# Half of a recurrent state transposed on VectorE and through DRAM instead of on TensorE, with five PSUM banks for gates and one for transposes

## The chip, the cores and the metric

The kernel runs on one core of a Trainium2 chip. The metric is device time in microseconds (us) of one execution. Three executions of the kernel before gave 2820.95, 2821.49 and 2822.5 us; the median is 2821.49 us. A further execution was profiled: its program took 2821.51 us and the span of its records, on which all sums below are made, is 2819.7 us.

## The reference, cut to what matters

There are B = 128 graphs of N = 128 nodes with D = 256 features, in float32. Three attention layers come first (each: layer norm, ReLU, masked softmax attention, ELU, added to the input), then one gated graph layer of three steps. The change lies in the gated layer alone:

```
h = relu(layernorm(x))
A = (adj != 0)
for i in range(3):
    m    = h @ weight[i]                      # 128 x 256 per graph
    aggr = A.T @ m                            # messages summed over neighbours
    gi, gh = aggr @ w_ih.T + b_ih, h @ w_hh.T + b_hh
    r = sigmoid(i_r + h_r); z = sigmoid(i_z + h_z)
    n = tanh(i_n + r * h_n)
    h = (1 - z) * n + z * h
x = x + h
```

The kernel multiplies `weight[i]` into `w_ih` once at the start (`wc`), so that a step is: sum `h` over neighbours (`ag`), then products of `ag` with `wc` and of `h` with `w_hh`, then the gates.

## The kernel before, in words

**Tiling.** The 128 graphs are cut into 33 groups: 2 graphs, 31 times 4 graphs, 2 graphs (`SIZES`, line 213). A group of 4 graphs has 512 columns, one PSUM bank of float32. The state `h` is kept with features on the partitions, in two halves of 128 features (`h0`, `h1`; the code's `k` where it is read and `c` where it is written), each 128 x 512.

**One gated step** (`step`, line 738). The products with weights take `h` as it lies. The sum over neighbours needs the nodes on the partitions, so for steps 1 and 2 each half is transposed first: `node_major` (line 726) makes one TensorE transpose per graph into a PSUM bank `hnp`, ScalarE copies the bank to `hn` (line 762), four TensorE products of `hn` with the adjacency `am` fill the bank `agp` (line 773), and VectorE copies it to `ag` (line 781). For step 0 the node-major state is there already (`hn0`). In `half(c)` (line 784) each half of the new state takes four gate banks: `nn`, `r` and `z` start from `h` and `whh`, `r` and `z` are finished with `ag` and `wc`, `ni` is made from `ag` and `wc` alone (all line 751). ScalarE and VectorE then form the gates, and the last VectorE instruction (line 840) writes the new half `h`. All of half 0 precedes half 1 in the gate arithmetic, so `h0` of a step is ready some 10 us before `h1`.

**PSUM.** The eight banks are shared out in line 231: two for attention (`gat`), four for gates and for the setup's products (`gru`), two for transposes and neighbour sums (`tr`).

**Transposes without TensorE.** The kernel already has one such way, `exchanged` (line 428): VectorE transposes the 32 x 32 blocks of a tile, one DMA writes the result to DRAM, and four DMAs (one for each 32 partitions) read the blocks back in their new places. It serves the attention weights (`tr_at`, `d_at`, `at`), the first state of a group (`tr_h`, `d_h`, `h`) and the last (`tr_o`, `d_o`, `o`), for the groups that `far` selects; the groups at the ends use TensorE.

**Order of the work.** Nothing is ordered by hand. Every instruction is given to a planner (`Plan`, line 40) with its engine, a cost, a rank and what it reads and writes. The planner lets the engines run in simulated time; whenever one is free it takes, of the instructions that could start within 0.1 us of the earliest, the one of lowest rank (lines 132 to 140). A buffer ring (an SBUF tag, a PSUM tag) holds an instruction back until its slot is free. A DMA costs SyncE 0.45 us and its data are taken to land a stated time later: the first argument of `load`. The result is one fixed order for each engine, TensorE's, VectorE's, ScalarE's and SyncE's (which issues all DMAs); on the chip each engine goes through its order and waits on semaphores. So a landing time in the code delays nothing by itself: it decides where the instructions that need the data are put. Ranks rise by 3 for each group; attention of a later group has a rank near that of the gated steps of an earlier one, and its TensorE work is what stands between the gated steps. Gate arithmetic is ranked 2 ahead (`quick`).

**Start.** Weights are transposed and multiplied on TensorE while the attention of the first two groups begins: `attention_weights` (line 280) forms `va` by VectorE products (line 294), TensorE transposes `vp` (line 299) and a ScalarE copy (line 306); the attention scores (line 483) wait for `va`. `mask` (line 316) transposes the node mask `nm` (line 320), and `transposed` (line 328) the weights (line 338).

Of the kernel before, what the change touches and what calls it, by code (L numbers as in the profile page):

```python
# [8 lines left out]
FT = mybir.dt.float32  # L9
# [5 lines left out]
P = 128  # L15
# [24 lines left out]
class Plan:  # L40
# [15 lines left out]
    def load(self, lands, rank, fn, **keys):  # L56

        op = self.add("SP", 0.45, rank, fn, **keys)
        op.lands = lands
        return op  # L60

    def add(self, engine, cost, rank, fn, reads=(), writes=(), after=(), takes=()):


        reads = [k if isinstance(k, tuple) else (k, None) for k in reads]
        writes = [k if isinstance(k, tuple) else (k, None) for k in writes]
        vals = list(dict.fromkeys(v for v, _ in reads + writes))
        vals += [v for v in dict.fromkeys(takes) if v not in vals]
        op = Op(engine, cost, rank, fn, vals)
        for v in vals:  # L70
            v.ops.append(op)

        def others(book, key):
            for part, ops in book.get(key[0], {}).items():
                if part is None or key[1] is None or part == key[1]:
                    yield from ops

        for key in reads:
            for d in others(self.writers, key):
                op.deps[d] = True  # L80
        for key in writes:
            for book in (self.writers, self.readers):
                for d in others(book, key):
                    op.deps.setdefault(d, False)
        for d in after:
            op.deps.setdefault(d, False)
        for v, part in writes:
            w, r = self.writers.setdefault(v, {}), self.readers.setdefault(v, {})
            if part is None:
                w.clear()  # L90
                r.clear()
            else:
                r.pop(part, None)
            w[part] = [op]
        for v, part in reads:
            if (v, part) not in writes:
                self.readers.setdefault(v, {}).setdefault(part, []).append(op)
        for d in op.deps:
            d.users.append(op)
        self.ops.append(op)  # L100
        return op
# [80 lines left out]
def kernel(  # L182
# [25 lines left out]
    nc = tc.nc  # L208
    B, N, D = x.shape
    KD = D // P  # L210
    G = 4
    FAR = 2
    SIZES = [2] + [G] * ((B - 4) // G) + [2]
    NG = len(SIZES)
# [13 lines left out]
    setup = ExitStack()  # L228
    su = setup.enter_context(tc.tile_pool(name="setup", bufs=2))
    rw_pool = []  # L230
    BANKS = {"gat": 2, "gru": 4, "tr": 2}

    plan = Plan()
    add, load = plan.add, plan.load
# [4 lines left out]
    def val(pool, tag, shape, name, bufs=2, dtype=FT, cut=None):  # L239

        def make():
            if pool is None and not rw_pool:
                setup.close()
                rw_pool.append(ctx.enter_context(tc.tile_pool(name="rw", bufs=2)))
            p = rw_pool[0] if pool is None else pool
            t = p.tile([P, *shape], dtype, tag=tag, name=name, bufs=bufs)
            return t if cut is None else t[:, :cut]
        return plan.val(pool, tag, bufs, make)
# [10 lines left out]
    def dve(cols):  # L259
        return 0.12 + cols / 1000  # L260

    def act(cols):
        return 0.25 + cols / 1400
# [52 lines left out]
    def mask():  # L316
        nm = val(su, "nm", [N], "nm")
        nmp = bank("gat", "nmp")
        load(2.6, SETUP, lambda: nc.sync.dma_start(nm.t[:B], nodemask), writes=[nm])
        add("PE", 0.11, SETUP, lambda: nc.tensor.transpose(nmp.t[:, :B], nm.t[:B], ident[:B, :B]),  # L320
            reads=[nm], writes=[nmp])
        add("ACT", act(P), SETUP, lambda: nc.scalar.copy(nmT.t, nmp.t[:, :B]),
            reads=[nmp], writes=[nmT])
# [4 lines left out]
    def transposed(src, dst, name):  # L328
        rows = src.shape[0] // P
        ld = val(su, "wld", [O3 // P, D], f"{name}_ld")  # L330
        load(2.6, SETUP, lambda: nc.sync.dma_start(
            ld.t[:, :rows], src.rearrange("(r p) d -> p r d", p=P)), writes=[ld])

        def part(k, r0, n):
            ps = bank("gru", f"{name}_{k}_{r0}")

            def turn(r):
                add("PE", 0.11, SETUP, lambda: nc.tensor.transpose(
                    ps.t[:, r * P : (r + 1) * P], ld.t[:, r0 + r, k * P : (k + 1) * P], ident
                ), reads=[ld], writes=[(ps, r)], takes=[dst])  # L340

            for r in range(n):
                turn(r)
            add("ACT", act(n * P), SETUP, lambda: nc.scalar.copy(
                dst.t[:, k, r0 * P : (r0 + n) * P], ps.t[:, : n * P]
            ), reads=[ps], writes=[(dst, (k, r0))])

        for k in range(KD):
            for r0 in range(0, rows, 4):
                part(k, r0, min(4, rows - r0))  # L350
# [77 lines left out]
    def exchanged(srcs, cut, dst, name, n, rank):  # L428

        kd = len(srcs)
        f = kd * n * 32
        tr = val(gw, f"tr{kd}", [Q, kd * G * 32], f"tr_{name}")
        d = plan.val(
            dram, f"d{kd}_{n}", 2,
            lambda: dram.tile([Q, 32, Q, f], FT, tag=f"d{kd}_{n}", name=f"d_{name}"),
        )

        def blocks(k):  # L440
            add("DVE", dve(n * P), rank, lambda: nc.vector.transpose(
                tr.t[:, :, :f].rearrange("p j (k b c) -> p k b j c", k=kd, b=n)[:, k],
                cut(k).rearrange("p b (j r) -> p b j r", j=Q),
            ), reads=[srcs[k]], writes=[(tr, k)], takes=[d, dst])

        for k in range(kd):
            blocks(k)
        load(2.8 if kd == 1 else 3.8, rank, lambda: nc.sync.dma_start(
            d.t.rearrange("q r j f -> (q r) j f"), tr.t[:, :, :f]), reads=[tr], writes=[d])

        def back(j):
            load(2.8 if kd == 1 else 3.8, rank, lambda: nc.sync.dma_start(
                dst.t[j * 32 : (j + 1) * 32, :, :f], d.t[:, :, j, :].rearrange("q r f -> r q f")
            ), reads=[d], writes=[(dst, j)])

        for j in range(Q):
            back(j)
# [246 lines left out]
    def gru(g, xt, am, hn0, h0):  # L704
# [7 lines left out]
        def state(tag, name, bufs=2):  # L712
            return val(None, tag, [T], name, bufs=bufs)
# [12 lines left out]
        def node_major(name, hv, k, rank, to):  # L726
            ps = bank("tr", f"hnp_{name}_{k}")

            def turn(b):
                add("PE", 0.11, rank, lambda: nc.tensor.transpose(  # L730
                    ps.t[:, b * P : (b + 1) * P], hv.t[:, b * P : (b + 1) * P], ident
                ), reads=[hv], writes=[(ps, b)], takes=[to])

            for b in range(n_g):
                turn(b)
            return ps

        def step(i):
            name = f"{g}_{i}"
            rank = 3.0 * g + i  # L740
            quick = rank - URGENT
            ag = [state(f"ag{k}", f"ag_{name}_{k}") for k in range(KD)]
            hn = [state(f"hn{k}", f"hn_{name}_{k}") for k in range(KD if i > 0 else 0)]

            def product(ps, c, w, v, k, start, stop, at, takes=(), after=after):
                def fn():
# [10 lines left out]
            def aggregate(k):  # L757

                if i > 0:
                    hv = hn[k]  # L760
                    hp = node_major(name, h[k], k, rank + 0.1 * k, hv)
                    add("ACT", act(TG), quick, lambda: nc.scalar.copy(hv.t[:, :TG], hp.t[:, :TG]),  # L762
                        reads=[hp], writes=[hv])
                ps = bank("tr", f"agp_{name}_{k}")
                t = ag[k]

                def part(b):
                    def fn():
                        if i > 0:
                            s = hv.t[:, b * P : (b + 1) * P]  # L770
                        else:
                            s = hn0.t[:, b, k * P : (k + 1) * P]
                        nc.tensor.matmul(  # L773
                            ps.t[:, b * P : (b + 1) * P], s, am.t[:, b, :], start=True, stop=True
                        )
                    add("PE", pe(P), rank + 0.1 * k, fn,
                        reads=[hv if i > 0 else hn0, am], writes=[(ps, b)], after=after, takes=[t])

                for b in range(n_g):
                    part(b)  # L780
                add("DVE", dve(TG), quick, lambda: nc.vector.tensor_copy(t.t[:, :TG], ps.t[:, :TG]),  # L781
                    reads=[ps], writes=[t])

            def half(c):
# [44 lines left out]
                def difference():  # L829
# [10 lines left out]
                add("DVE", dve(TG), quick, lambda: nc.vector.scalar_tensor_tensor(  # L840
                    hc.t[:, :TG], d.t[:, :TG], 0.5, n.t[:, :TG], op0=OP.mult, op1=OP.add
                ), reads=[d, n], writes=[hc])
                return hc

            return [half(c) for c in range(KD)]
# [78 lines left out]
```

## Time and profile before

| engine | busy us | share of the span | instructions |
|---|---|---|---|
| TensorE, matmuls | 2763.2 | 98% | 10021 |
| VectorE | 2142.3 | 76% | 5622 |
| ScalarE | 1234.5 | 44% | 2627 |
| GpSimd | 293.0 | 10% | 369 |
| 16 DMA engines, mean (queue of SyncE's DMAs) | | 22.5% | 197104 packets |

The page names engines by short names: PE is TensorE, PEld its weight loads, DVE VectorE, ACT ScalarE, SP SyncE. Every float32 product appears as two PE instructions, a transpose as one. The duration of a PE instruction includes latency that overlaps its neighbours: 792 instructions of 580 ns in each of six groups are more than the span holds. What one costs is read from the distance between the starts of successive ones in the timeline.

The granted TensorE clock is 0.994 of full speed over the span. In windows, PE is busy 59.05 of the first 90 us, 48.29 of the next 60, 147.65 of the 150 after that, 696.13 of 300 to 1000 us, all of 1000 to 2700 us, and 52.28 of the last 60 us.

### The profile page before, as it was taken

How to read it: one execution, taken by the hardware profiler on the slowest of the kernel's cores; microseconds unless marked ns; L12 is line 12 of the kernel's file. 1: busy time of each engine (PE TensorE's matmuls, PEld its weight loads, DVE VectorE, ACT ScalarE, POOL GpSimd, SP SyncE). 2: the span in 40 equal slices, each digit the busy share in tenths (PEclk: the TensorE clock that was granted, in tenths of full speed). 3: DMA queues.
4: the chain of work that ended last, by engine and by line, in shares of the span. 5: the costliest groups of instructions: out<-in, count | busy, mean ns of one | idle time of the engine just before them, and what ended most of it. 6: DMA issues, size and time to landing. Idle time of an engine off the chain costs nothing.

```text
span 2819.7 us, 32353 instructions
## 1 busy us (share of the span) xinstructions
PE 2763.2 (98%) x10021; PEld 1615.4 (57%) x10021; DVE 2142.3 (76%) x5622; ACT 1234.5 (44%) x2627; POOL 293.0 (10%) x369
## 2 busy tenths in 40 slices
PE   6889999999999999999999999999999999999998
PEld 4755555555555555555555555555555555555556
DVE  6879888778787778777778777777777787776543
ACT  4444444444444444444444444444444444444322
POOL 1111111101110101110110110110110110100000
PEclk9999999999999999999999999999999999999999
DMA  3123212222212222112222122222122222122100
GB/s 100 38 67 87 77 51 83 75 79 79 56 50 75 77 78 79 49 56 75 75 79 75 50 60 75 71 79 76 48 62 77 72 79 70 40 58 60 47 30 12
DMA packets 197277, 185.24 MB, mean 66 GB/s; under 512 B 33776, under 2 KB 165872, under 8 KB 197104
## 3 DMA queue, kind: packets, MB, share of 16 engines
q1 hardware_dynamic: 197104, 183.17, 22.5%
q8 instruction: 79, 1.29, 0.2%
q14 instruction: 94, 0.77, 0.1%
HBM read 109.65 MB, written 73.46 MB: 65 GB/s over the span
## 4 chain that ended last, share of the span: by engine, by line
PE 93%; DVE 5%; DMA 1%; ACT 1%; issue 0%; SPq 0%; POOL 0%; DVEq 0%; ACTq 0%
PE r L751 22%; PE z L751 22%; PE hp L614 11%; PE ni L751 11%; PE nn L751 11%; PE ahp L595 6%; PE agp L773 6%; PE hnp L730 2%; DVE scr L483 1%; PE wcp L370 0%; DVE st L413 0%; DVE em L525 0%; DVE xo L630 0%; DVE xo L632 0%; DMA whh_ld<-in_L_gnn_w_hh_dram 0%
## 5 line engine op out<-in xcount | busy, mean ns | idle before, releaser
L751 PE MATMUL nn<-h,whh 128*128 128x512 f32 (+1 forms) x792 | 395.8, 581 | 10.2 <-DMA h<-d_h 8.4
L751 PE MATMUL r<-ag,wc 128*128 128x512 f32 (+1 forms) x792 | 397.0, 583 | 2.5 <-DVE ag L781 2.5
L751 PE MATMUL z<-ag,wc 128*128 128x512 f32 (+1 forms) x792 | 394.3, 579 | 0.0
L751 PE MATMUL r<-h,whh 128*128 128x512 f32 (+1 forms) x792 | 394.2, 580 | 0.0
L751 PE MATMUL ni<-ag,wc 128*128 128x512 f32 (+1 forms) x792 | 394.1, 579 | 0.0
L751 PE MATMUL z<-h,whh 128*128 128x512 f32 (+1 forms) x792 | 394.1, 579 | 0.0
L614 PE MATMUL hp<-w,ah 128*128 128x256 f32 x1536 | 363.3, 382 | 0.2
L808 ACT ACTIVATE r<-r,brz 128x512 f32<-128x512 f32 (+1 forms) x198 | 133.1, 672 | 483.7 <-PE r L751 483.2
L614 PEld LDWEIGHTS hp<-w,ah 128*128 128x128 f32 x1536 | 281.1, 191 | 40.3 <-ACT ah L602 5.3
L483 DVE SCALAR_TENSOR_TENSOR scr<-xn,va 128x256 f32<-128x256 f32 x732 | 265.9, 422 | 29.5 <-ACT xn L475 28.6
L811 DVE SCALAR_TENSOR_TENSOR n<-r,wn 128x512 f32<-128x512 f32 (+1 forms) x198 | 132.6, 669 | 179.0 <-ACT r L808 178.5
L751 PEld LDWEIGHTS r<-ag,wc 128*128 128x128 f32 x792 | 148.2, 190 | 186.6 <-issue 155.3
L751 PEld LDWEIGHTS r<-h,whh 128*128 128x128 f32 x792 | 150.4, 190 | 178.2 <-issue 174.9
L751 PEld LDWEIGHTS z<-h,whh 128*128 128x128 f32 x792 | 149.9, 190 | 177.5 <-issue 158.2
L773 PEld LDWEIGHTS agp<-am,hn 128*128 128x128 f32 x1536 | 203.4, 191 | 57.8 <-issue 37.8
L751 PEld LDWEIGHTS ni<-ag,wc 128*128 128x128 f32 x792 | 145.6, 190 | 147.8 <-issue 128.7
L628 ACT ACTIVATE t<-hp 128x512 f32<-128x512 f32 x192 | 104.4, 594 | 286.9 <-PE hp L614 283.5
L751 PEld LDWEIGHTS z<-ag,wc 128*128 128x128 f32 x792 | 145.6, 190 | 147.3 <-issue 145.9
L773 PE MATMUL agp<-am,hn 128*128 128x128 f32 x1536 | 208.8, 276 | 4.9 <-ACT hn L762 3.6
L751 PEld LDWEIGHTS nn<-h,whh 128*128 128x128 f32 x792 | 142.6, 191 | 121.9 <-issue 105.9
L525 DVE SCALAR_TENSOR_TENSOR em<-er,e,cap 128x128 f32<-128x128 f32 x366 | 156.8, 484 | 67.6 <-DMA er<-de 67.6
L494 POOL TENSOR_SCALAR xo<-xo 128x1024 f32<-128x1024 f32 (+1 forms) x66 | 73.3, 1111 | 1292.6 <-DMA out_dram<-xo 589.3
(90 smaller groups left out, 3662.3 us busy)
## 6 DMA issues: line engine op xcount, KB each, us to landing
er<-de SPq DMA_DIRECT2D x90, 256.0 KB, 4.1
d_at<-tr_at SPq DMA_DIRECT2D x90, 256.0 KB, 2.0
at<-d_at SPq DMA_DIRECT2D x360, 64.0 KB, 2.0
x<-in_x_dram SPq DMA_DIRECT2D x31, 512.0 KB, 4.0
d_h<-tr_h SPq DMA_DIRECT2D x31, 512.0 KB, 4.9
h<-d_h SPq DMA_DIRECT2D x124, 128.0 KB, 3.4
out_dram<-xo SPq DMA_DIRECT2D x31, 512.0 KB, 2.9
d_o<-tr_o SPq DMA_DIRECT2D x30, 512.0 KB, 4.3
```

Source lines behind the costliest of these rows:

```text
L483: add("DVE", dve(D), rank, lambda: nc.vector.scalar_tensor_tensor(scr.t, xn.t[:, b, :], 1.0 if far else rs.t[:, b : b + 1], VA[l].t[:, s, ...
L494: add("POOL", 0.14 + n * D / 1070, rank, lambda: nc.gpsimd.tensor_scalar(xo.t, xt.t, 1.0, -1.0, op0=OP.mult, op1=OP.add), reads=[xt], writ ...
L525: add("DVE", dve(P) + (0.15 if far else 0.05), rank, lambda: nc.vector.scalar_tensor_tensor(em.t[:, b, :], e2_row(b), e.t[:, 0, b : b + 1] ...
L595: add("PE", pe(P), rank, lambda: nc.tensor.matmul(summed(ps, b), xn.t[:, b, k * P : (k + 1) * P], turned_weights(b), start=True, stop=True ...
L614: add("PE", pe(D), rank, lambda: nc.tensor.matmul(hp.t[:, b * D : (b + 1) * D], ah.t[:, k, c * P : (c + 1) * P], W[l].t[:, k, :], start=(k ...
L628: power = add("ACT", act(T), rank, lambda: nc.scalar.activation(t.t, hp.t, AF.Exp), reads=[hp], writes=[t])
L730: add("PE", 0.11, rank, lambda: nc.tensor.transpose(ps.t[:, b * P : (b + 1) * P], hv.t[:, b * P : (b + 1) * P], ident), reads=[hv], writes ...
L751: nc.tensor.matmul(o, w.t[:, k, c * P : (c + 1) * P], m, start=start, stop=stop)
L773: nc.tensor.matmul(ps.t[:, b * P : (b + 1) * P], s, am.t[:, b, :], start=True, stop=True)
L808: add("ACT", act(TG) + 0.1, quick, lambda: nc.scalar.activation(r.t[:, :TG], pr.t[:, :TG], AF.Tanh, bias=brz.t[:, cr : cr + 1], scale=0.5) ...
L811: add("DVE", dve(TG), quick, lambda: nc.vector.scalar_tensor_tensor(n.t[:, :TG], r.t[:, :TG], 1.0, wn.t[:, :TG], op0=OP.add, op1=OP.mult), ...
```

## The change

Five edits are made.

1. Of six PSUM banks that gates and transposes share, gates get five instead of four and transposes one instead of two.
2. A new function, `turned_state`, transposes one half of the state without TensorE: one VectorE transpose of 32 x 32 blocks (128 x 512), one DMA of 256 KB to DRAM in pieces of 512 B, four DMAs of 64 KB back, one for each 32 partitions, in pieces of 128 B. The planner is told 3.0 us for the landing of the first and 6.0 us (`LANDS`) for each of the four.
3. It is called at the end of half 0 of steps 0 and 1, for groups 2 to 30 (all of four graphs): 58 times.
4. Where it was called, the next step leaves out the four TensorE transposes of half 0, their PSUM bank and the ScalarE copy. Half 1 goes as before, and so do groups 0, 1, 31 and 32.
5. In the setup, the planner is told other landing times: 8.0 us instead of 2.6 for the node mask, 8.0 for the two large weights and 4.0 for the three small ones, instead of 2.6.

```diff
+    LANDS = 6.0
-    BANKS = {"gat": 2, "gru": 4, "tr": 2}
+    BANKS = {"gat": 2, "gru": 5, "tr": 1}
...
-        load(2.6, SETUP, lambda: nc.sync.dma_start(nm.t[:B], nodemask), writes=[nm])
+        load(8.0, SETUP, lambda: nc.sync.dma_start(nm.t[:B], nodemask), writes=[nm])
...
-        load(2.6, SETUP, lambda: nc.sync.dma_start(
+        load(8.0 if rows > KD else 4.0, SETUP, lambda: nc.sync.dma_start(
             ld.t[:, :rows], src.rearrange("(r p) d -> p r d", p=P)), writes=[ld])
...
+    def turned_state(src, dst, name, n, rank):
+        tr = val(gw, "trs", [G, P], f"tr_{name}", cut=n)
+        d = plan.val(
+            dram, f"ds_{n}", 2, lambda: dram.tile([n, P, P], FT, tag=f"ds_{n}", name=f"d_{name}")
+        )
+        add("DVE", dve(n * P), rank, lambda: nc.vector.transpose(
+            tr.t.rearrange("p b j -> p (b j)"), src.t[:, : n * P]
+        ), reads=[src], writes=[tr], takes=[d, dst])
+        load(3.0, rank, lambda: nc.sync.dma_start(d.t.rearrange("b p f -> p b f"), tr.t),
+            reads=[tr], writes=[d])
+        def back(j):
+            load(LANDS, rank, lambda: nc.sync.dma_start(
+                dst.t[j * 32 : (j + 1) * 32, : n * P].rearrange("c (m r) -> c m r", r=32),
+                d.t[:, :, j * 32 : (j + 1) * 32].rearrange("b (q c) r -> c (b q) r", q=Q),
+            ), reads=[d], writes=[(dst, j)])
+        for j in range(Q):
+            back(j)
...
+        ahead = []
...
-            hn = [state(f"hn{k}", f"hn_{name}_{k}") for k in range(KD if i > 0 else 0)]
+            hn = [
+                ahead[0] if k == 0 and ahead else state(f"hn{k}", f"hn_{name}_{k}")
+                for k in range(KD if i > 0 else 0)
+            ]
...
-                    hp = node_major(name, h[k], k, rank + 0.1 * k, hv)
-                    add("ACT", act(TG), quick, lambda: nc.scalar.copy(hv.t[:, :TG], hp.t[:, :TG]),
-                        reads=[hp], writes=[hv])
+                    if k == 0 and ahead:
+                        ahead.clear()
+                    else:
+                        hp = node_major(name, h[k], k, rank + 0.1 * k, hv)
+                        add("ACT", act(TG), quick, lambda: nc.scalar.copy(
+                            hv.t[:, :TG], hp.t[:, :TG]), reads=[hp], writes=[hv])
...
+                if c == 0 and i < STEPS - 1 and FAR <= g < NG - FAR:
+                    ahead.append(state("hn0", f"hn_{g}_{i + 1}_0"))
+                    turned_state(hc, ahead[0], f"hn_{g}_{i + 1}", n_g, quick)
                 return hc
```

## The prediction

> **What bounds the kernel now.** I read the page's first part and its chain of work first, then the PE timeline of one group from the middle, then the waits of PE, then the start. Engine shares and the chain:
>
> ```profile
> PE 2763.2 (98%) x10021; PEld 1615.4 (57%) x10021; DVE 2142.3 (76%) x5622; ACT 1234.5 (44%) x2627; POOL 293.0 (10%) x369
> PE 93%; DVE 5%; DMA 1%; ACT 1%; issue 0%; SPq 0%; POOL 0%; DVEq 0%; ACTq 0%
> ```
>
> A busy PE need not be PE at its peak, so the next view must show it. In the PE timeline the distance between starts is what an instruction costs. At the first hand-over between two gated steps of one group:
>
> ```profile
> 1390.18 1.02 PE L751 MATMUL nn<-h,whh 128*128 128x512 f32 x2
> 1391.05 1.02 PE L751 MATMUL r<-h,whh 128*128 128x512 f32 x2
> 1391.90 1.02 PE L751 MATMUL z<-h,whh 128*128 128x512 f32 x2
> 1392.76 0.60 PE L730 MATMUL hnp<-ident,h 128*128 128x128 f32 x4
> 1393.20 1.46 PE L614 MATMUL hp<-w,ah 128*128 128x256 f32 x6
> 1394.50 1.05 PE L773 MATMUL agp<-am,hn 128*128 128x128 f32 x8
> 1395.39 2.32 PE L614 MATMUL hp<-w,ah 128*128 128x256 f32 x10
> 1397.55 1.02 PE L751 MATMUL nn<-h,whh 128*128 128x512 f32 x2
> ```
>
> The reader is to see that no line has an idle time: attention work (hp) fills the hand-over. A gate product takes 0.86 us from start to start, four transposes 0.44 us (1392.76 to 1393.20), a neighbour sum 0.89, sixteen hp 3.46, sixteen ahp 1.79. A group of four graphs needs 72 gate products (61.9), 3 times 16 hp (10.4) and 16 ahp (5.4), six neighbour sums (5.3) and four sets of transposes (1.8): 84.8 us. The chain of work in order of time shows successive groups 84.9 us apart (ahp at 1364.34, again at 1449.24). So between about 300 and 2700 us **PE's throughput sets the time**, with nothing to spare: 1 us of PE work less per group is 1 us less, if PE is still never kept waiting.
>
> The start is different. Its waits, of PE and of DVE:
>
> ```profile
> PE nmp L320 <- DMA nm<-in_nodemask_dram: 13.3, 1, 13.3
> PE nn L751 <- DMA h<-d_h: 8.4, 1, 8.4
> DVE scr L483 <- ACT va L306: 8.5, 1, 8.5
> ```
>
> PE's first instruction, the mask's transpose, waits until 13.29 us for its load, and the first transpose of whh until 15.45. The four vp transposes that va needs stand behind them, though their inputs were made on DVE by 9.3 us (timeline); so DVE idles from 11.3 to 19.87. The 8.4 us later on is group 1's first state, which comes late out of the same stretch.
>
> **What the Trainium skill says.** "TensorE: Matmul & The Clock Gate", Part 4 (PE-mode transpose), gives about 275 ns for a transpose in a kernel's context; the trace has 273, but only 0.11 us of each is PE's own time here, and that is what I use. "VectorE: DVE Perf Modes", The three transpose paths, says that VectorE transposes 32 x 32 blocks only, so blocks must be moved by something else: in this kernel already by DMAs (tr_at, d_at, at). "DMA: Bandwidth & Descriptors", Specifications, states that pieces under 512 B cause read-modify-write. The trace of before doesn't show it as a delay: at<-d_at lands 2.0 us after issue both with 512 B pieces (64 KB) and with 256 B pieces (32 KB). The same page, Anatomy of one DMA, says that a DMA's wait is made on the issuing sequencer; the trace agrees, SyncE waiting 123.1 us in 89 waits for d_at before it issues at.
>
> **The change part by part.** Rows used:
>
> ```profile
> L730 PE MATMUL hnp<-ident,h 128*128 128x128 f32 x524 | 79.6, 273 | 3.0 <-DVE h L840 3.0
> L762 ACT COPY hn<-hnp 128x512 f32<-128x512 f32 x124 | 72.0, 581 | 123.0 <-PE hnp L730 122.9
> L441 DVE STREAM_TRANSPOSE tr_at<-em 128x512 f32<-128x512 f32 x90 | 64.0, 711 | 3.0
> d_at<-tr_at SPq DMA_DIRECT2D x90, 256.0 KB, 2.0
> at<-d_at SPq DMA_DIRECT2D x360, 64.0 KB, 2.0
> out_dram<-xo SPq DMA_DIRECT2D x31, 512.0 KB, 2.9
> ```
>
> *Removed from PE.* 29 groups, two hand-overs each, four transposes: 232 of 524. 58 x 0.44 = **25.5 us**, all in the stretch where PE sets the time. The group's period goes from 84.9 to 84.0 us.
>
> *Removed from ACT.* 58 copies of 0.58 us, 34 us. ACT is 44% busy; counted as nothing.
>
> *Added on DVE.* 58 x 0.71 = 41 us, 76% to 78% of the span. Each is ranked with the gates, so it stands behind h0 and ahead of half 1's gate arithmetic; what it delays by 0.7 us is h1 or an attention step. At the hand-over shown h1 was written at 1393.2 and first used at 1397.55, so 4 us of attention work on PE cover it. Counted as nothing.
>
> *Added on SyncE and the DMA engines.* A write takes 0.34 us to issue and four reads 1.75 us (timeline, L448 and L452): 58 x 2.1 = 121 us of SyncE. Queued behind the new wait for the write are de, er, at and the loads of x and adj; DVE's em waits for er, PE's ahp for at. A wait of 2 to 3 us, 58 times, in an order made with a longer landing: counted as nothing, at worst part of the stalls below. Packets: by the trace's packet records one of 512 B takes 28 ns in its engine, of 256 B 19, of 16 B 9; 128 B isn't there, I take 13 by interpolation. A write gives 32 packets per engine (0.9 us), the reads together 128 (1.7 us): 58 x 2.6 = 151 us, 5% of the span on top of 22.5%.
>
> *The new path and its wait.* Before, h0 was finished at 1383.42 (DVE h L840) and agp of half 0 began at 1394.50, 11.1 us later; at the group's other hand-over 1412.03 and 1421.91, 9.9 us. The new path: transpose 0.71; write 2.5 (2.0 by d_at, 2.9 by out, which has as many packets); four issues 1.75; the last landing 2.2 (at's 2.0 plus 24 more packets of 13 ns less at's larger ones): 7.2 us. Upper end: write 3.0 and reads of 56 ns a packet, double the 512 B price for the unshown read-modify-write: 7.2 for all four plus 1.8 fixed, in all 12.7. The planner assumes 0.63 + 0.2 + 0.45 + 3.0 + 4 x 0.45 + 6.0 = **12.1 us** and puts agp where that fits; after 1394.5 there is 4.7 us of hp and h1 products that it can put ahead. Against 12.1 the stall per hand-over is 0 at 7.2 and 0.6 at 12.7. It can't be negative, because agp isn't moved ahead of its place when data come early. I take 0; the upper end is 58 x 0.6 = 35 us.
>
> *Banks.* With one tr bank, hnp of half 1, agp 0 and agp 1 of a step must each be copied out before the next begins: some 1.5 to 1.8 us a turn (PE 0.44 or 0.89, copy 0.58 or 0.69, hand-offs), 5 us of the 28 us of a step, so the bank suffices, and the planner can place other work between. The fifth gate bank lets a product of half 1 begin early, which is that work. In steady state 0 (bounds 0 to 0.3 us x 66, 20 us). At the start, hTp and agp of group 0 line up in one bank: +1 us. At the end groups 31 and 32 keep all transposes with one bank: +1 us for four hand-overs (bounds 0 to 4).
>
> *Setup's landing times.* With nm and whh put 8 us after issue, the planner puts them behind vp and the first score rows. Then va is ready near 10.5 us instead of 19.7, and DVE's 8.5 us of idle time goes. Not all comes through: whh really lands at 15.4 and wih some 2 us later, and the transposes of both (24 x 0.21 us at the start's clock) still stand ahead of group 0's first atp, which came at 25.86 and would come near 20. I take **6 us** (bounds 0 and 9), carried to the end because PE is full from 300 us on.
>
> Sum on the span: 2819.7 - 25.5 - 6 + 1 + 1 = 2790.2. The runs lie 1.8 us above the span (2821.5 to 2819.7): **2792 us**.
>
> **The rivals.** *A, saving whole, start not better.* The two groups' attention is bound by DVE, near full from 20 to 60 us, or PE is blocked as before by whh. 2792 + 6 = 2798. For it: whh's real landing. Against it: DVE's gap has one cause.
>
> *B, bank turns.* The single tr bank makes PE wait where the planner has nothing to place: 0.3 x 66 = 20 us given back, 2812. For it: three turns now go through one bank. Against it: 4 us of slack at the hand-over shown.
>
> *C, slower: late node-major state.* In PE's fixed order agp waits for hn0 itself. If the four reads of 128 B pieces with the wait on SyncE take more than the planner's 12.1 us from h0, every us of excess is paid 58 times. From (25.5 + 4) / 58 = 0.5 us of excess the kernel is slower; at 1.2 us it costs 70, and 2792 + 70 = 2862. For it: 128 B pieces appear nowhere in the trace, and larger loads do land late (adj, 256 KB in 512 B pieces, 4.7 us behind x). Against it: packets of 256 B and 16 B are cheap.
>
> *D, doesn't do what it says:* all 29 groups have four graphs and the condition holds for each, so I give that no chance of its own.
>
> **How the numbers follow.** Forecast, 2780 to 2796: 0.55. A, to 2803: 0.18. B, to 2817: 0.14. C: 0.13. No change that a measurement could tell from none is within 0.2%, 5.6 us: 2815.8 to 2827.1; the tails of B and C give it 0.05. Faster 0.84, slower 0.11. The range 2780 to 2817 leaves out C and a little at the low end, where the full 9 us of the start and the 6 us that PE idles between 150 and 1000 us would go.
>
> **What would show it.** Right: hnp 292 instead of 524, groups 84.0 us apart, no PE wait for hn at agp, DVE's wait for va gone, and first gate products before 83 us. Wrong: PE agp waiting for the DMA of hn (C); PE hnp or agp waiting for DVE ag or ACT hn (B); the same start (A). The prediction fails if the new path takes over 12 us.

## The result, and the profile after

Six executions of the changed kernel took 2795.6 to 2801.3 us, median **2798.9 us**; six of the kernel before, taken with them, 2820.95 to 2828.55, median 2821.93. The ratio is 0.9915, with a 95% interval of 0.9902 to 0.9928: the change saves 23.0 us. The prediction was 2792 in a range of 2780 to 2817, so the direction and the range hold, and 6.5 us of the forecast saving of 29.5 did not come. Where they went is what most of the experiments are about.

The profiled execution of the changed kernel was the slowest of the six, with a span of 2799.5 us. Its engine shares and its chain, as the page gives them:

```profile
PE 2744.8 (98%) x9789; PEld 1592.6 (57%) x9789; DVE 2188.9 (78%) x5680; ACT 1207.8 (43%) x2569; POOL 293.9 (10%) x369
PE 84%; DVE 9%; DMA 3%; ACT 2%; SPq 1%; issue 1%; POOL 0%; DVEq 0%; ACTq 0%
```

PE has 232 instructions fewer and is still busy for 98% of a shorter span. But it holds 84% of the chain instead of 93%: in some places the chain now leaves PE for VectorE and the DMAs. The groups that the change touches (busy us, mean ns, idle time before them), and then its two DMAs (KB each, median us to landing):

```profile
L753 PE MATMUL hnp<-ident,h 128*128 128x128 f32 x292 | 45.2, 275 | 3.4 <-DVE h L872 3.0 <-DVE ag L813 0.3
L467 DVE STREAM_TRANSPOSE tr_hn<-h 128x512 f32<-128x512 f32 x58 | 41.3, 711 | 2.0
L794 ACT COPY hn<-hnp 128x512 f32<-128x512 f32 x66 | 38.6, 585 | 82.4 <-PE hnp L753 82.3
```

```profile
d_hn<-tr_hn SPq DMA_DIRECT2D x58, 256.0 KB, 2.3
hn<-d_hn SPq DMA_DIRECT2D x232, 64.0 KB, 2.2
```

The counts are those of the diff: 292 transposes on PE, 58 on VectorE, 66 copies. The hand-over that the prediction showed looks like this now, in the PE timeline:

```profile
1378.78 1.02 PE L780 MATMUL nn<-h,whh 128*128 128x512 f32 x2
1379.64 1.02 PE L780 MATMUL r<-h,whh 128*128 128x512 f32 x2
1380.50 1.02 PE L780 MATMUL z<-h,whh 128*128 128x512 f32 x2
1381.35 1.89 PE L637 MATMUL hp<-w,ah 128*128 128x256 f32 x8
1383.08 1.05 PE L805 MATMUL agp<-am,hn 128*128 128x128 f32 x8
1383.97 1.89 PE L637 MATMUL hp<-w,ah 128*128 128x256 f32 x8
1385.70 1.02 PE L780 MATMUL nn<-h,whh 128*128 128x512 f32 x2
```

The line of four transposes is gone, no line has an idle time, and the starts stand as far apart as before. VectorE's transpose for this hand-over begins at 1372.32, so the neighbour sum (agp) begins 10.8 us later. PE's waits between 150 and 2700 us, the longest totals (us in total, times, longest):

```profile
PE nn L780 <- DVE h L872: 6.0, 6, 2.8
PE agp L805 <- DVE ag L813: 1.8, 1, 1.8
PE agp L805 <- ACT hn L794: 1.4, 2, 0.7
PE ahp L618 <- DMA at<-d_at: 1.2, 1, 1.2
```

There is no wait for the DMA hn<-d_hn. What has grown are the waits of nn for h: 6.0 us in six waits, where the same view of the kernel before has 0.6 us in two. At the start, the first product of a gated step in the PE timeline:

```profile
77.64 0.60 PE L780 MATMUL nn<-h,whh 128*128 128x256 f32 x2
```

It stood at 83.59 us before.

### The profile page after: what moved, and what is told of

It is laid out like the page before. It is cut to its first block, busy times and chain, and to the rows that moved or that the text cites. A ratio compares the mean times of both kernels' runs of the same rounds, so it can differ in the third digit from the quotient of the medians.

```text
span 2799.5 us, 32211 instructions
## 1 busy us (share of the span) xinstructions
PE 2744.8 (98%) x9789; PEld 1592.6 (57%) x9789; DVE 2188.9 (78%) x5680; ACT 1207.8 (43%) x2569; POOL 293.9 (10%) x369
## 3 DMA queue, kind: packets, MB, share of 16 engines
q1 hardware_dynamic: 350224, 213.60, 28.1%
## 4 chain that ended last, share of the span: by engine, by line
PE 84%; DVE 9%; DMA 3%; ACT 2%; SPq 1%; issue 1%; POOL 0%; DVEq 0%; ACTq 0%
PE r L780 20%; PE z L780 20%; PE hp L637 11%; PE ni L780 10%; PE nn L780 10%; PE agp L805 5%; PE ahp L618 5%; DVE scr L506 1%; DMA d_o<-tr_o 1%; PE hnp L753 1%; DVE d L869 1%; DVE n L848 1%; DVE h L872 1%; DVE n L843 1%; DMA d_h<-tr_h 1%
## 5 line engine op out<-in xcount | busy, mean ns | idle before, releaser
L637 PE MATMUL hp<-w,ah 128*128 128x256 f32 x1536 | 374.1, 383 | 0.7 <-ACT ah L625 0.5
L566 ACT ACTIVATE em<-em,nmx 128x128 f32<-128x128 f32 x384 | 149.5, 391 | 187.8 <-DVE nmx L562 187.7
L618 PEld LDWEIGHTS ahp<-at,xn 128*128 128x128 f32 x1536 | 188.8, 194 | 47.7 <-issue 40.4
```

The costliest lines, as they stand in the source:

```text
L566: add("ACT", 0.42, rank, lambda: nc.scalar.activation(em.t[:, b, :], em.t[:, b, :], AF.Exp, bias=nmx.t[:, b : b + 1], accum_out=sm.t[:, b ...
L618: add("PE", pe(P), rank, lambda: nc.tensor.matmul(summed(ps, b), xn.t[:, b, k * P : (k + 1) * P], turned_weights(b), start=True, stop=True ...
L637: add("PE", pe(D), rank, lambda: nc.tensor.matmul(hp.t[:, b * D : (b + 1) * D], ah.t[:, k, c * P : (c + 1) * P], W[l].t[:, k, :], start=(k ...
```

## The experiments

All twelve kernels were timed in rounds with the kernel before on the same chip. "Saved" is the median of before in the same series (2821.7 to 2822.97 us) less the kernel's own. Profiles are of one execution each, so their times can differ from these medians by a few us.

| kernel | median us | ratio to before, 95% interval | saved us |
|---|---|---|---|
| the change | 2798.9 | 0.9915 [0.9902, 0.9928] | 23.0 |
| e1_setup | 2818.79 | 0.9987 [0.998, 0.9994] | 3.9 |
| e2_turn_only | 2811.61 | 0.9965 [0.9952, 0.9977] | 11.1 |
| e3_banks_only | 2824.15 | 1.0007 [0.9998, 1.0015] | -1.5 |
| e4_left_out | 2795.96 | 0.9905 [0.9892, 0.9919] | 26.7 |
| e5_turn_banks | 2805.56 | 0.9938 [0.9926, 0.9951] | 16.7 |
| e6_lands | 2803.78 | 0.9931 [0.9917, 0.9944] | 18.5 |
| e7_er_margin | 2866.79 | 1.0152 [1.0138, 1.0166] | -44.5 |
| e8_both_halves | 2806.3 | 0.9944 [0.9932, 0.9957] | 16.0 |
| e9_x_on_act | 2798.03 | 0.9916 [0.9902, 0.9929] | 23.7 |
| e10_er_on_pool | 2805.61 | 0.9944 [0.9931, 0.9958] | 16.1 |
| e11_no_path | 2791.18 | 0.9886 [0.9873, 0.99] | 31.8 |
| e12_path_unused | 2798.82 | 0.9918 [0.9905, 0.9932] | 24.2 |

### The parts alone

**e1_setup**: the kernel before with edit 5 alone.

```diff
-        load(2.6, SETUP, lambda: nc.sync.dma_start(nm.t[:B], nodemask), writes=[nm])
+        load(8.0, SETUP, lambda: nc.sync.dma_start(nm.t[:B], nodemask), writes=[nm])
...
-        load(2.6, SETUP, lambda: nc.sync.dma_start(
+        load(8.0 if rows > KD else 4.0, SETUP, lambda: nc.sync.dma_start(
```

> The kernel before with the setup's five landing times alone. If the shortfall of the whole change (23 us instead of 29.5) lies in the start, this gives 0 to 2 us. If the start gives what its trace suggests (first gate product at 77.6 us instead of 83.6), this gives about 6 us: 2815 to 2816 us.

Measured: 3.9 us saved; the first gate product begins at 79.69 us, 3.9 earlier than before, and the last gate instruction of VectorE 3.7 earlier. So the start's gain is carried to the end.

**e2_turn_only**: the change without edits 1 and 5.

```diff
-    BANKS = {"gat": 2, "gru": 5, "tr": 1}
+    BANKS = {"gat": 2, "gru": 4, "tr": 2}
...
-        load(8.0, SETUP, lambda: nc.sync.dma_start(nm.t[:B], nodemask), writes=[nm])
+        load(2.6, SETUP, lambda: nc.sync.dma_start(nm.t[:B], nodemask), writes=[nm])
...
-        load(8.0 if rows > KD else 4.0, SETUP, lambda: nc.sync.dma_start(
+        load(2.6, SETUP, lambda: nc.sync.dma_start(
```

> The new path alone: banks 4 and 2, setup's landing times as before. Theory S (SyncE: what is given back is er and at issued late behind the new DMAs): 25.5 us less work on PE minus some 7 us of stalls, about 2803 us, with DVE waits for er longer than before and PE waits for DVE h. Theory T (one bank for transposes gives it back): the whole 25.5 us come through here, about 2796 us.

Measured: 11.1 us saved, less than half of what the removed transposes were priced at. A hand-over of it, in the PE timeline:

```profile
1389.85 1.95 PE L805 MATMUL agp<-am,hn 128*128 128x128 f32 x16
1391.63 1.02 PE L780 MATMUL nn<-h,whh 128*128 128x512 f32 x2
1393.26 1.13 PE L780 MATMUL nn<-h,whh 128*128 128x512 f32 x2 [0.60 <-DVE h L872]
```

and its largest wait between 150 and 2700 us:

```profile
PE nn L780 <- DVE h L872: 11.2, 24, 1.3
```

Both neighbour sums stand one behind the other, nothing of the attention stands between them and nn, and nn's second half is 0.60 us ahead of h1.

**e3_banks_only**: the kernel before with edit 1 alone.

```diff
-    BANKS = {"gat": 2, "gru": 4, "tr": 2}
+    BANKS = {"gat": 2, "gru": 5, "tr": 1}
```

> Five gate banks and one transpose bank alone; transposes of both halves stay on PE, so three and four turns of a step go through the one bank. Theory T: slower than before by 5 to 20 us, with PE waits of hnp and agp for ACT hn and DVE ag. Theory S: within 2 us of before.

Measured: 1.5 us slower, with an interval that holds no change. In its profile VectorE writes the last h of group 1 2.9 us later than before, the first h of group 31 2.5 us later and the first of group 32 4.9 us later: what it loses stands at the two ends of the program.

**e5_turn_banks**: the change without edit 5 (the same two load lines as in e2_turn_only; the banks stay at five and one).

> The new path with five gate banks and one transpose bank, setup's landing times as before. The new path alone gave 2811.6 us and its PE waits 24 times for the second half of the state (nn waits for DVE h, 11.2 us). Theory G (a fifth gate bank is what fills that hand-over, since half 0's transposes no longer stand there): 2802 to 2804 us, and these waits nearly gone. Theory H (banks alone cost 1.5 us, so they don't matter, and the rest of the whole change's gain is the start): 2811 to 2813 us.

Measured: 16.7 us saved, 5.6 more than e2_turn_only. The waits of nn fall from 24 to 7:

```profile
PE nn L780 <- DVE h L872: 5.0, 7, 1.6
```

So the banks are worth nothing alone and 5.6 us beside the new path: with a fifth bank the planner again puts attention work between the sums and the products of h1. That this order, and not the bank as such, is the cause is argued from the timelines of e2_turn_only and of the change. Edit 5 on top of e5_turn_banks saves another 6.3 us (16.7 to 23.0).

### What the removed work is worth, and what the new path costs

**e4_left_out**: the kernel before, without half 0's transposes, bank and copy in the 29 groups.

```diff
+            kept = hn[1:] if FAR <= g < NG - FAR else hn
...
-                    hv = hn[k]
-                    hp = node_major(name, h[k], k, rank + 0.1 * k, hv)
-                    add("ACT", act(TG), quick, lambda: nc.scalar.copy(hv.t[:, :TG], hp.t[:, :TG]),
-                        reads=[hp], writes=[hv])
+                    if k == 0 and FAR <= g < NG - FAR:
+                        hv = h[k]
+                    else:
+                        hv = hn[k]
+                        hp = node_major(name, h[k], k, rank + 0.1 * k, hv)
+                        add("ACT", act(TG), quick, lambda: nc.scalar.copy(
+                            hv.t[:, :TG], hp.t[:, :TG]), reads=[hp], writes=[hv])
...
```

> The kernel before, with the transposes and the copy of half 0 left out for groups 2 to 30 and nothing in their place: the neighbour sum of half 0 reads the state as it lies. Banks 4 and 2, setup as before. This is the price of the removed PE work without the new path: 25.5 us if a transpose costs PE 0.11 us, so 2796 us. If it is much less, the transposes were partly hidden, and the new path gave nothing back; if it is 25 and the new path alone gives less, the difference is the path's own cost.

Measured: 26.7 us saved. The price of 0.44 us for four transposes, read from the distance of starts, is confirmed within the noise (25.5 forecast); the sum of durations would have given 58 x 4 x 0.273 = 63 us.

**e11_no_path**: the changed kernel with the path left out.

```diff
...
-                    if k == 0 and ahead:
-                        ahead.clear()
+                    if k == 0 and FAR <= g < NG - FAR:
+                        hv = h[0]
...
-                if c == 0 and i < STEPS - 1 and FAR <= g < NG - FAR:
-                    ahead.append(state("hn0", f"hn_{g}_{i + 1}_0"))
-                    turned_state(hc, ahead[0], f"hn_{g}_{i + 1}", n_g, quick)
```

**e12_path_unused**: the changed kernel with the whole path kept and its result unread.

```diff
                         ahead.clear()
+                        hv = h[0]
```

> The changed kernel (banks five and one, setup's landing times new) with the new path left out and nothing in its place: the neighbour sum of half 0 reads the state as it lies. It is what the change would give if the path were free. By the sum of the parts measured so far (26.7 us for the transposes, 4 to 7 for the setup, minus 1.5 for the banks) 2789 to 2793 us. If it is near 2799, the path costs nothing and banks or setup give back what is missing.

> The changed kernel with the new path kept whole (transpose on VectorE, write, four reads) but its result not used: the neighbour sum of half 0 reads the state as it lies, so nothing waits for the path. If the cost of the path is its place on VectorE, SyncE and the DMA engines (theory S), this takes as long as the changed kernel, 2797 to 2801 us. If it is the wait for the data at the hand-over, which takes the place of the transposes there, this takes as long as the kernel without the path.

Measured: 2791.18 and 2798.82 us. Without the path the kernel takes what was forecast for the change (2792). With the path present but unread it takes what the change takes (2798.9). Since PE waits for hn's data in neither, the 7.6 us between the two kernels are the price of the path's place among the other work. The windows of e11_no_path (us; busy us and instructions of PE, PEld, DVE, ACT and POOL; clock, DMA share, GB/s):

```profile
245.00:815.00 570.00, 567.38 (x2030) 327.40 (x2029) 463.18 (x1230) 256.12 (x548) 66.73 (x80) 1.00 0.25 72
815.00:2500.00 1685.00, 1684.78 (x5936) 962.72 (x5935) 1347.66 (x3468) 741.08 (x1563) 181.54 (x220) 1.00 0.23 69
```

of e12_path_unused:

```profile
245.00:815.00 570.00, 560.04 (x1984) 321.35 (x1983) 465.38 (x1234) 253.03 (x541) 66.92 (x80) 1.00 0.31 83
815.00:2500.00 1685.00, 1684.94 (x5933) 961.93 (x5932) 1359.27 (x3504) 738.88 (x1563) 180.07 (x220) 1.00 0.30 81
```

and of the changed kernel:

```profile
245.00:815.00 570.00, 560.91 (x1977) 321.32 (x1976) 465.78 (x1227) 251.96 (x539) 65.48 (x80) 0.99 0.31 83
```

From 815 to 2500 us PE is idle for less than 0.3 us in the first two and 1.0 us in the change (its line there has 1684.02 us busy). Between 245 and 815 us PE is busy 7.3 us less in e12_path_unused than in e11_no_path. PE's waits in that stretch, e11_no_path first:

```profile
PE nn L778 <- DVE h L870: 2.0, 5, 0.8
PE ahp L618 <- DMA at<-d_at: 0.4, 1, 0.4
```

```profile
PE nn L780 <- DVE h L873: 8.2, 8, 2.5
PE ahp L618 <- DMA at<-d_at: 1.6, 1, 1.6
```

6.2 us more for h and 1.2 for at make 7.4, what PE lost in this stretch. How much of the lateness of h comes from VectorE's own transposes and how much from SyncE and the DMA engines was not tried. The order of all engines is planned anew when the path is taken out, and also when its result is left unread, and these kernels can't part that from the path itself.

How far ahead of the kernel before each profiled execution is, by the start of VectorE's last gate instruction (the one that writes h; us), shows the stages apart:

| | end of group 1, the start | first h of group 31, the steady part | last h |
|---|---|---|---|
| forecast of the change | 5 | 30.5 | 29.5 |
| e11_no_path | 5.8 | 31.2 | 29.5 |
| e12_path_unused | 7.7 | 25.7 | 23.9 |
| the change | 9.1 | 21.9 | 20.3 |

In e11_no_path each stage comes as forecast: 25.4 us from the groups with the path's edits, for 25.5. Against it the path costs 7.4 us between group 1 and group 31 in e12_path_unused and 12.6 in the profiled change, which was the slowest of its six executions; an earlier start wins back 1.9 and 3.3 us of that. Why the start differs between kernels with the same setup was not followed.

### One of these waits, followed to its source

In the changed kernel's profile the longest wait for h is at 534.72 us. Four views of it: SyncE's timeline, VectorE's, PE's, and two windows, of which the second is the stretch of reduced clock (columns as above).

```profile
515.77 0.40 SPq L668 DMA_DIRECT2D x<-in_x_dram  x1
517.19 0.38 SPq L470 DMA_DIRECT2D d_hn<-tr_hn  x1
...
523.79 1.91 SPq L474 DMA_DIRECT2D hn<-d_hn  x4
525.75 1.91 SPq L453 DMA_DIRECT2D h<-d_h  x4
527.71 0.43 SPq L530 DMA_DIRECT2D er<-de  x1
```

```profile
531.84 0.78 DVE L548 SCALAR_TENSOR_TENSOR em<-er,e,cap 128x128 f32<-128x128 f32 x2 [2.76 <-DMA er<-de]
...
533.98 0.69 DVE L872 SCALAR_TENSOR_TENSOR h<-d,n 128x512 f32<-128x512 f32 x1
```

```profile
530.86 1.02 PE L780 MATMUL nn<-h,whh 128*128 128x512 f32 x2
534.72 2.08 PE L780 MATMUL nn<-h,whh 128*128 128x512 f32 x2 [2.83 <-DVE h L872]
536.59 1.91 PE L780 MATMUL r<-h,whh 128*128 128x512 f32 x2
538.29 1.92 PE L780 MATMUL z<-h,whh 128*128 128x512 f32 x2
```

```profile
530.48:533.89 3.41, 1.41 (x7) 0.58 (x6) 2.02 (x4) 1.31 (x3) 0.00 (x0) 1.00 0.07 22
533.89:540.72 6.83, 6.00 (x10) 2.79 (x11) 6.18 (x23) 1.84 (x7) 0.00 (x0) 0.50 0.00 0
```

Read from the top: the path's write d_hn is issued 1.4 us after a load of 512 KB (x) and lands 6.5 us after its issue, against a median of 2.3. SyncE waits for it, and four reads of hn, four of h and then er are queued behind. er, needed for a mask of another group, is issued at 527.71; VectorE waits 2.76 us for it in front of the arithmetic of h1; PE waits 2.83 us for h1. Then PE runs at half pace: nn to r takes 1.87 us instead of 0.86, r to z 1.70, and the granted clock is 0.50 for 6.83 us. That costs some 2.7 us beyond the wait. Here the path's cost is the order of a queue that it shares with er, and it reaches PE by way of VectorE. What made the write late these views don't show; the load of x ahead of it is the suspect of the next experiment.

**e9_x_on_act**: the changed kernel, x and adj loaded from ScalarE's queue.

```diff
-        load(4.8, rank - 4, lambda: nc.sync.dma_start(
+        load(4.8, rank - 4, lambda: nc.scalar.dma_start(
...
-        load(4.8, rank - 3.6, lambda: nc.sync.dma_start(
+        load(4.8, rank - 3.6, lambda: nc.scalar.dma_start(
```

> The changed kernel with the loads of x and adj issued by ScalarE instead of SyncE, at the same place in the planner's order. Theory S (near 530 us the path's write lands 6.6 us after issue, behind a 512 KB load of x issued 1.4 us ahead of it on the same queue, and er is issued late behind it): write lands within 3 us everywhere, the 2.83 us wait of PE and its 2.7 us at half clock go, 2793 to 2796 us. If the event comes from the planned order itself, the same within 1 us; if ScalarE is held up by its waits for x's buffers, slower by 2 us or more.

Measured: 2798.03 us, the same as the change. At this hand-over PE waits 1.65 us and keeps its pace. But d_hn still takes 5.4 us, again 1.4 us behind the load of x, which ScalarE now issues. So SyncE's queue is not what makes the write late. In both kernels the two writes of the whole program that follow a load of x within 1.6 us are late, 3.1 and 6.5 us in the change and 3.1 and 5.4 here, so x's bytes remain the suspect; that is not shown. And in e5_turn_banks, whose x stands on SyncE's queue, PE's wait here is 1.56 us, so the fall to 1.65 need not come from this edit.

**e10_er_on_pool**: de and er issued from GpSimd's queue.

```diff
-            load(2.2, rank, lambda: nc.sync.dma_start(de.t, e.t[:, 1, :n]),
+            load(2.2, rank, lambda: nc.gpsimd.dma_start(de.t, e.t[:, 1, :n]),
...
-            load(4.6, rank, lambda: nc.sync.dma_start(
+            load(4.6, rank, lambda: nc.gpsimd.dma_start(
```

> The changed kernel with de and er issued by GpSimd instead of SyncE, so that er stands behind none of the new path's DMAs. Theory S: DVE's waits for er shrink in the stretch to 1000 us, the wait near 530 us goes, 2793 to 2796 us. If it is the traffic on the DMA engines and not the queue, er is as late as before and the time stays within 1 us of 2798.9. If GpSimd's issue is slower than SyncE's, er is later everywhere, and the kernel is slower.

Measured: the wait of 2.83 us falls to 0.17. er now lands 11.4 us after the path's write is issued, for 14.6 in the change, and VectorE doesn't wait for it there. This supports the step from er's place on SyncE to the wait. Yet the kernel is 6.7 us slower than the change. In its profile the end of group 1 comes 5.4 us later than in the change; why was not followed. And VectorE's waits for er between 245 and 815 us add up to 19.3 us for 15.5 in the change. So the remedy is none.

**e7_er_margin**: er told to the planner as landing later, so that its users are planned later.

```diff
-            load(4.6, rank, lambda: nc.sync.dma_start(
+            load(7.4, rank, lambda: nc.sync.dma_start(
```

> The changed kernel with one number changed: the planner is told 7.4 us instead of 4.6 for the landing of er, so VectorE's em stands later in its order. Theory S (SyncE issues er late behind the new path's DMAs, em blocks VectorE, the second half of the state comes late, PE waits): the wait of PE nn for DVE h near 530 us (2.83 us, and 2.7 us more at a lower clock) goes, and the kernel is 3 to 6 us faster, 2793 to 2796. Otherwise the same within 1 us, with the waits elsewhere.

Measured: 2866.79 us, over 70 us above what was expected, and the slowest kernel of all. VectorE's waits for er are gone but for one of 0.8 us, but PE's, between 150 and 2700 us, have grown:

```profile
PE nn L780 <- DVE h L872: 33.4, 42, 1.2
PE ahp L618 <- DMA at<-d_at: 13.2, 12, 1.4
PE hnp L753 <- DVE ag L813: 13.0, 13, 1.6
```

Its hand-overs have no attention work between the sums and nn, and VectorE waits 412.3 us for ScalarE's t where it waits 66.7 in the change. Why the planner, told of a later er, moved the attention out of the hand-overs was not settled.

### How much room the path has

**e6_lands**: the reads told as landing 3.5 us after issue (they measure 2.2).

```diff
-    LANDS = 6.0
+    LANDS = 3.5
```

> The changed kernel with one number changed: the planner is told 3.5 us for the landing of the four reads instead of 6.0 (measured: 2.2 median, 4.2 longest). If the planner's long landing time holds the neighbour sum back and costs, this is faster by 2 us or more. If PE is full anyway, it is within 2 us of 2798.9; if the margin covered late landings, PE agp now waits for the DMA of hn, and it is slower.

Measured: 18.5 us saved, 4.5 less than with 6.0. The stated landing that is nearer to the real one is the worse: PE's waits at agp for DVE ag rise from 1.8 us in one wait to 6.6 in five. That the planner puts the sums closer to one another is argued, not shown. In its profile the end of group 1 comes 2.3 us later than in the change, so part of the loss may be the start, where the path has no part.

**e8_both_halves**: half 1 takes the path as well (LANDS 3.5).

```diff
+            mine = list(ahead)
+            ahead.clear()
...
-                ahead[0] if k == 0 and ahead else state(f"hn{k}", f"hn_{name}_{k}")
+                mine[k] if mine else state(f"hn{k}", f"hn_{name}_{k}")
...
-                    if k == 0 and ahead:
-                        ahead.clear()
-                    else:
+                    if not mine:
...
-                if c == 0 and i < STEPS - 1 and FAR <= g < NG - FAR:
+                if i < STEPS - 1 and FAR <= g < NG - FAR:
-                    ahead.append(state("hn0", f"hn_{g}_{i + 1}_0"))
-                    turned_state(hc, ahead[0], f"hn_{g}_{i + 1}", n_g, quick)
+                    ahead.append(state(f"hn{c}", f"hn_{g}_{i + 1}_{c}"))
+                    turned_state(hc, ahead[c], f"hn_{g}_{i + 1}_{c}", n_g, quick)
```

> The changed kernel with the second half of the state also sent by the new path (no transposes on PE in groups 2 to 30, 58 more), and 3.5 us told for the reads. It takes 25.5 us more of work off PE. If the hand-over has room for a path of 6.7 us from h1 too (before, agp of half 1 began some 9 us after h1): 2773 to 2780 us. If not, PE waits at agp for the DMA of hn in each hand-over: over 2799 us from 0.45 us a hand-over on.

Measured: 16.0 us saved, though PE has only 60 transposes left. agp waits for the DMA of hn once, 0.6 us, so the path is fast enough even for half 1. The waits that eat the gain are agp for DVE ag (12.6 us in 32 waits: a sum waits until VectorE has copied the sum before it out of the one bank) and nn for h (14.9 us in 29).

## Why the prediction was right, and where its sum was off

The direction, the range and the mechanism are right. The number is less so: 2798.9 lies above the band of 2780 to 2796 that the prediction gave its own forecast, and in that of rival A, whose mechanism is not what happened.

**PE's throughput sets the time.** Right. After 815 us successive groups follow 84.1 us apart in e11_no_path and 84.2 in the change (84.0 forecast, 84.9 before), and leaving the transposes out saves 26.7 us for 25.5 forecast. Two side remarks on the way to that price don't hold. The six gate groups' durations, 792 of 580 ns each, are 2756 us and so not yet more than the span; only with hp's 1536 of 382 ns are they. And the 275 ns that the prediction quotes for a transpose stands on its page beside a figure for bf16, so that the trace has 273 for float32 confirms nothing. Neither entered the sum.

**The new path and its wait.** Right, and rival C falls. In the median the transpose takes 0.71 us, the write until the first read is issued 2.3, the four issues 1.4 and the landing of the last read 2.4. From the transpose's start to the last landing it is 6.9 us in the median and 11.1 at the longest, for 7.2 forecast and 12.1 planned. The 128 B pieces, whose price was open, took 12.6 ns a packet for the 13 taken. Per byte that is dearer than the 29 ns of a 512 B packet (10 B per ns against 18), but a step that the read-modify-write of the Trainium skill for pieces under 512 B ("DMA: Bandwidth & Descriptors", Specifications) would make is not to be seen: 16 B take 8.6 ns, 256 B 19. The DMA queue's share went from 22.5% to 28.1%, 5.6 points for 5 forecast.

**Setup's landing times.** Right: 6.3 us on top of the other edits for 6 forecast, and 3.9 alone, with intervals that don't part the two; the first gate product came 5.95 us earlier than before, ahead of 83 us as said. The mechanism is the one that was named: va is copied from 10.19 us on instead of 19.16, and the first atp begins at 18.80 us, for near 20 forecast. So rival A falls, though its number, 2798, is the one that was measured: that is chance, a better start and a dearer path. What remains of VectorE's gap for va is, in the whole execution's waits:

```profile
DVE scr L506 <- ACT va L307: 0.4, 1, 0.4
```

**Added on SyncE, the DMA engines and VectorE.** This is the term that was mis-sized: "counted as nothing" for VectorE because "4 us of attention work on PE cover it", and for SyncE "counted as nothing, at worst part of the stalls below". It is 7.6 us (e11_no_path to e12_path_unused). The cover was read at one hand-over at 1390 us and taken for all 58. After 815 us it holds in e12_path_unused; between 245 and 815 us it is thinner, and h, ag, at or ah comes 0.2 to 2.8 us late, eight times in the change and ten in e12_path_unused. With that term the sum is 2799.6, for 2798.9 measured. In the change itself the sum closes less neatly: its profiled execution loses 12.6 us in the steady part and has 3.3 us more from the start than e11_no_path. Of the 12.6, 6.5 are idle time of PE between 245 and 815 us and 2.7 the reduced clock; most of the rest lies after 815 us, where groups follow 0.15 us farther apart than in e11_no_path, almost without idle time. What that is stays open.

**Banks.** "In steady state 0" is right for the edit alone (e3_banks_only) and leaves out what it does beside the path: without the fifth bank 5.6 us of the gain are lost. The sum had the right number for the kernel as a whole, since it assumed hand-overs filled with attention work; it did not see that without the fifth bank they don't stay so. The 1 us taken for groups 31 and 32 is 2.3 in the profiles of the change and of e3_banks_only, between the first h of group 31 and that of group 32. Rival B's mechanism, turns of the single bank, is there in e8_both_halves, and in the change it amounts to waits for DVE ag of 1.8 and 0.3 us; those for ACT hn are 1.4 us, less than the 2.4 of before.

## What to carry to other kernels

On a full engine, price removed work by the distance between starts, then ask of every stage, not only of the steady one, what covers the work that replaces it. To price a replacement, keep it and leave its result unread: what the kernel still pays is its place in the queues, what it stops paying is the wait. Where a planner makes the order, what the new order costs is in both. In such an order a stated landing time is a lever on the order and not a description of the chip; the truer number can be the slower one, and 2.8 us more, told for the loads of er, moved the end by 68.

## What the runs showed of the hardware that was not expected

An idle time of 2.83 us was enough to halve PE's pace for some 5 us (starts 0.86 us apart for each instruction instead of 0.43), while one of 1.65 us in the same place (e9_x_on_act) cost its own length alone. The Trainium skill, "TensorE: Matmul & The Clock Gate", Why this matters for your kernels, asks for no idle gaps above some 3 us; here a gap slightly under that already paid.

The length of the gap alone does not decide it. In e2_turn_only a gap of 2.15 us before 411.82 was followed by half the clock; in e6_lands one of 2.69 us before 625.90 was not. In the clock records of all fourteen traces every change of the clock stands a whole number of slots of 3.41 us after the first. The slots around these two gaps, e2_turn_only first (columns as above):

```profile
407.89:411.30 3.41, 1.16 (x8) 0.97 (x8) 3.31 (x10) 0.57 (x1) 0.35 (x1) 1.00 0.16 62
411.30:414.72 3.42, 2.90 (x4) 1.36 (x5) 2.03 (x10) 0.69 (x1) 1.72 (x2) 0.50 0.30 89
621.50:624.91 3.41, 1.71 (x10) 0.88 (x8) 3.34 (x10) 2.09 (x4) 0.00 (x0) 1.00 0.34 113
624.91:628.33 3.42, 2.43 (x12) 1.71 (x13) 3.31 (x13) 0.31 (x1) 0.00 (x0) 1.00 0.08 21
```

What goes with the slower clock is how little PE is busy within one slot: 1.16 us of 3.41 here and 1.41 in the change (530.48 to 533.89) are followed by 0.50, and 1.71 in e6_lands, whose longer gap is shared by two slots, by 1.00. In e12_path_unused a gap of 2.46 us leaves 1.66 us busy in its slot, and the clock stays too. From 150 us on this parts all slots at full clock of the fourteen traces without an exception: 16 with at most 1.41 us busy are followed by half the clock, 10,866 with at least 1.57 us are not. In the first 150 us the border is less sharp (1.50 to 1.70). The ends of PE's instructions are modelled, so the border is an estimate. No run was made to test it.

The six runs of the change spread over 5.7 us. The clock event need not be why: the 18 runs of e1_setup, which has no such wait, spread over 6.4.
